# A cross-attention and mixture-of-experts kernel on one core: the order of all steps made anew, without a limit on how close GpSimd's transfers stand

## The chip, the core and the metric

The kernel runs on one core of a Trainium2 chip. Its engines run beside each other, each in the order of its own queue, and wait for one another by semaphores: TensorE (PE; its weight loads are shown as PEld), VectorE (DVE), ScalarE (ACT), GpSimd (POOL) and SyncE (SP), which here issues transfers only. GpSimd issues the indirect transfers, whose target rows are read from memory. The metric is the device time of one execution in microseconds (us), less is better. A profile is one more execution, recorded instruction by instruction.

## What is computed

A layer norm, cross-attention of 2 x 1024 tokens to 2 x 154 context rows with 16 heads of 16, a residual sum, a second layer norm, and a mixture of 8 experts of which each token takes the best two. All is in 32-bit floats. The reference, cut:

```python
x = x + attention(layernorm(x), ctx, ctx, Wq, bq, Wk, bk, Wv, bv, Wo, bo)
x = x + ffn(layernorm(x), router_w, w1, w2)

def ffn(x, router_w, w1, w2):            # 2048 tokens of 256
    probs = softmax(x @ router_w.T)      # 8 experts
    vals, idx = top_k(probs, 2)
    out = zeros_like(x)
    for eid in range(8):
        w = sum(where(idx == eid, vals, 0), axis=-1)
        out = out + w[:, None] * (gelu(x @ w1[eid].T) @ w2[eid].T)   # 256 -> 1024 -> 256
    return out
```

## The kernel before

**Stages.** The 2048 tokens lie in four blocks of 512 (numbers 0 to 3). For each block there is attention: `prep_norm`, `flip_half` and `prep_q` make the queries; `maxima` (L618 on TensorE, L625 on VectorE) finds each row's largest score; `drop` sends these by SyncE through a small DRAM buffer into the queries' spare rows (L642, L645); `exps` and `last_exps` make the exponentials (scores on TensorE L657 and L674, exponentials on ScalarE L663 and L680); `values` (L695, L703), `divide`, and `project` (L735, L742) finish it, and `project` also stores the block's sum into `out`. Then the block's tokens are normed again into two buffers `xn` of half a block each (`second_norm` L767), and `logits`, `share`, `choose` and `place` find each token's two experts and its row in a table `row_d` in DRAM. `pack` (L776) puts the shares beside the rows in `xn`.

**The scatter.** `record.n.i` takes the 128 tokens i of block n: VectorE casts their two row numbers (L867), and GpSimd issues two indirect transfers that write the 128 rows of 1,088 bytes from `xn` into `row_d` (L874). So a block has four `record` steps and eight transfers. `fill` writes rows of nobody behind each expert's last row, also from GpSimd. A later fetch of rows waits for all scatters ahead of it in the program, and a later scatter for the reads of the fetches ahead of it. Rows of `xn` can't be written again until the scatters have read them.

**The experts.** The table is worked through in tiles of 128 rows, all of one expert. `plan.1` picks the first nine tiles from the counts of blocks 0 and 1, `plan.0` the others from all four; its last part also plans "quarter tiles", of four groups of 32 rows with an expert each, which take up what is left over (L913 to L945). For tile j SyncE fetches the expert's weights w1 (`fetch_weights`, L1100; for quarter tiles L1112) and the rows (`fetch_rows`, L1124; L1128 for quarters), TensorE turns the rows (`flip_rows`, L1137), VectorE copies the result to `xgT` (L1140), `expand` is the first matmul (L1181, for quarters L1195) with a GELU on ScalarE (L1186), and `contract` the second (L1247), after which VectorE weighs the result into one of three buffers `ag` (L1273) and GpSimd adds its rows into `out` by an indirect transfer (L1276). w1 has room for five tiles, rows for three, `xgT` for two. The experts' second weights w2 lie in a buffer for all eight (`load_w2`, L281); its last two places serve as scratch for the attention before they are loaded.

**The order.** The steps are generators: each `yield` ends a part. A list `ORDER` of 710 words, written out by hand or by a planner outside the file, names the step whose next part is issued next. As TensorE, VectorE, ScalarE and SyncE take their instructions in that order, the list sets each queue. GpSimd does so only up to the step `release`; after it, its own order is chosen when the kernel is built, from the same program. TensorE's results go to PSUM, with three places of one kind ("two", for `maxima` and `exps`, two places each, and `last_exps` and `expand`, one each) and two of another ("one", for most other steps). After `ORDER` a loop (`tiles`) goes on from tile 13 to the last, the same in both kernels.

The loop that issues the list:

```python
    for word in ORDER.split():
        name, *args = word.split(".")
        advance(name, *[int(a) if a.isdigit() else a for a in args])
```

Of the kernel before, what the change touches and what calls it, by code (L numbers as in the profile page):

```python
# [52 lines left out]
warm first_moments.0 first_moments.0 first_moments.0 loads.x1 biases first_moments.0  # L53
first_scale.0 biases prep_norm.0 prep_norm.0 prep_norm.0 prep_norm.0 loads.wq first_moments.1
constants flip_context.1 flip_context.0 first_moments.1 flip_context.1 flip_context.0
first_moments.1 flip_half.0.0 flip_half.0.0 flip_half.0.1 flip_half.0.1 keys.0 prep_q.0.0
first_moments.1 loads.x3 loads.bo first_scale.1 loads.wv keys.0 last_context.0 loads.wo
last_context.1 keys.0 keys.1 first_offset.1 prep_q.0.0 first_moments.3 prep_q.0.0
first_moments.3 prep_norm.1 keys.1 maxima.0.0 maxima.0.0 keys.1 first_offset.0 maxima.0.0
last_values.1 prep_norm.1 load_w2.4 last_values.1 maxima.0.1 prep_norm.1 last_values.1  # L60
maxima.0.1 loads.bias loads.rw first_moments.3 prep_q.0.1 clear_last prep_q.0.1 loads.x2
more_keys.0 maxima.0.1 maxima.0.2 maxima.0.2 prep_q.0.1 more_keys.1 maxima.0.3 load_w2.1
context_values.0 context_values.1 maxima.0.3 prep_norm.1 context_values.0 maxima.0.2 release
context_values.0 maxima.0.3 context_values.1 flip_half.1.0 drop.0.0 context_values.1
first_moments.2 maxima.0.4 flip_half.1.0 drop.0.0 flip_half.1.1 flip_half.1.1 flip_output
more_keys.0 flip_output maxima.0.4 prep_q.1.0 last_values.0 prep_q.1.0 first_moments.2
prep_q.1.0 maxima.0.4 first_moments.3 exps.0.0 exps.0.0 maxima.0.5 maxima.0.5 maxima.0.5
exps.0.0 centred_router last_values.0 maxima.0.6 maxima.0.6 last_values.0 exps.0.1 maxima.0.6
exps.0.1 centred_router maxima.0.7 maxima.0.7 values_bias values_bias maxima.0.7 exps.0.1
drop.0.1 first_moments.2 prep_q.1.1 first_scale.3 prep_q.1.1 last_exps.0.0 maxima.1.0  # L70
output_router last_exps.0.0 prep_q.1.1 maxima.1.0 more_keys.1 maxima.1.1 maxima.1.0
output_router values.0.0 first_offset.3 maxima.1.1 first_moments.2 drop.0.1 values.0.0
values.0.0 values.0.0 maxima.1.1 first_scale.2 exps.0.2 exps.0.2 first_offset.2 exps.0.2
own_logits.0 values.0.0 own_logits.0 prep_norm.3 prep_norm.3 maxima.1.2 maxima.1.2 output_bias
prep_norm.2 maxima.1.3 maxima.1.2 last_exps.0.1 maxima.1.3 maxima.1.3 prep_norm.2 exps.0.3
prep_norm.2 drop.1.0 drop.1.0 prep_norm.2 own_logits.1 last_exps.0.1 output_bias own_logits.1
flip_half.2.0 flip_half.2.0 output_bias divide.0.0 output_bias exps.0.3 exps.0.3 values.0.1
divide.0.0 values.0.1 values.0.1 values.0.1 exps.1.0 flip_half.2.1 exps.1.0 maxima.1.4
values.0.1 divide.0.1 exps.1.0 maxima.1.4 prep_norm.3 divide.0.1 maxima.1.5 maxima.1.5
project.0.1 maxima.1.4 maxima.1.6 maxima.1.5 maxima.1.6 flip_half.2.1 exps.1.1 maxima.1.6  # L80
exps.1.1 maxima.1.7 prep_q.2.0 exps.1.1 maxima.1.7 last_exps.1.0 maxima.1.7 add_bias.0 drop.1.1
drop.1.1 prep_q.2.0 last_exps.1.0 project.0.1 maxima.2.0 prep_q.2.0 project.0.0
second_moments.0.1 maxima.2.0 maxima.2.1 maxima.2.0 second_moments.0.1 project.0.0 maxima.2.1
prep_norm.3 load_w2.2 maxima.2.1 load_w2.5 values.1.0 values.1.0 second_moments.0.0 values.1.0
values.1.0 exps.1.2 exps.1.2 maxima.2.2 second_moments.0.0 logits.0 values.1.0 exps.1.2
maxima.2.2 maxima.2.3 prep_q.2.1 maxima.2.2 logits.0 last_exps.1.1 maxima.2.3 second_scale.0
prep_q.2.1 load_w2.3 clear_last prep_q.2.1 own_logits.2 maxima.2.3 second_scale.0 drop.2.0
add_bias.1 logits.0 last_exps.1.1 divide.1.0 own_logits.2 logits.0 divide.1.0 exps.1.3 share.0
values.1.1 share.0 exps.1.3 values.1.1 exps.1.3 share.0 drop.2.0 values.1.1 values.1.1 exps.2.0
second_norm.0 choose.0 last_exps.2.0 exps.2.0 exps.2.0 choose.0 place.0 maxima.2.4 values.1.1  # L90
place.0 last_exps.2.0 maxima.2.4 maxima.2.4 flip_half.3.0 flip_half.3.0 flip_half.3.1 maxima.2.5
flip_half.3.1 pack.0 prep_q.3.0 record.0.0 maxima.2.5 maxima.2.5 divide.1.1 maxima.2.6
record.0.0 maxima.2.6 exps.2.1 exps.2.1 maxima.2.6 prep_q.3.0 divide.1.1 maxima.2.7 exps.2.1
prep_q.3.0 maxima.2.7 project.1.1 maxima.2.7 maxima.3.0 drop.2.1 record.0.1 record.0.1
project.1.1 logits.1 add_bias.2 second_norm.0 project.1.0 drop.2.1 maxima.3.0 second_moments.1.1
logits.1 maxima.3.1 maxima.3.0 second_moments.1.1 project.1.0 record.0.2 second_moments.1.0
# [1409 lines left out]
```

## Time and profile before

| | us |
|---|---|
| median of 3 runs | 423.14 |
| lowest and highest run | 419.65, 423.66 |
| the profiled execution | 419.35 |
| its span, first to last instruction | 417.6 |
| its TensorE busy, VectorE busy | 396.0, 209.4 |
| granted TensorE clock | 0.995 |

The page says how long each engine was busy, cuts the span into 40 slices of some 10.4 us with a digit for the busy tenths of each, and lists groups of instructions with what ended the idle time ahead of them. A timeline has start, duration, engine, line, operation, output and inputs, how many were merged, and in brackets the idle time ahead and its releaser. A list of waits has total, number of times, and longest. The attention of the four blocks takes the span's first 150 us, the experts the rest; choosing and scattering of blocks 2 and 3 lie beside the first experts' tiles, up to 215 us.

Transfers in `row_d` issued by GpSimd (L874), in the view of that line: 32 of rows and two of filler, 957 to 1502 ns each, 962 in the middle.

### The profile page before, as it was taken

To read this page: it belongs to the slowest core of one execution; us is meant where nothing else is said; L and a number is where in the kernel's file an instruction comes from. 1 tells how busy PE (TensorE), PEld (TensorE's weight loads), DVE (VectorE), ACT (ScalarE), POOL (GpSimd) and SP (SyncE) were. 2 spreads that over 40 slices of the span, in tenths; PEclk is the share of its full clock that TensorE was granted. 3 is DMA by queue.
4 is the path that set the end of the run, shared out by engine and by line. 5 is a ranking of instruction groups with operands and counts; after the bars stand their busy time and mean duration, and the time that the engine had idled before them with its cause. 6 is when DMAs were issued, how large, how long until landed. Compare 5 with 4: busy or idle time off the path is not lost. (4 is left out here: it accounts for less than half of the span.)

```text
span 417.6 us, 8418 instructions
## 1 busy us (share of the span) xinstructions
PE 396.0 (95%) x3018; PEld 285.2 (68%) x3018; DVE 209.4 (50%) x608; ACT 125.0 (30%) x223; POOL 112.8 (27%) x146
## 2 busy tenths in 40 slices
PE   7999999999989979999989999999999999999990
PEld 6554444335324349999979999689968977896890
DVE  5765787888888785545202313532451424234300
ACT  2556654275263446431121112111111111111110
POOL 8500080203223303345541122211311222213121
PEclk9999999999999999999999999999999999999997
DMA  7700000801456369775949988798689679876211
GB/s 242 305 10 7 3 9 8 316 9 35 167 160 221 96 229 321 237 214 156 281 100 281 316 242 242 210 368 231 174 263 366 175 199 305 301 205 200 55 19 18
DMA packets 35870, 76.19 MB, mean 182 GB/s; under 512 B 6023, under 2 KB 15921, under 8 KB 34801
## 3 DMA queue, kind: packets, MB, share of 16 engines
q1 hardware_dynamic: 28960, 66.10, 48.1%
q0 software_dynamic: 6384, 8.92, 10.2%
q8 instruction: 27, 0.44, 0.4%
q10 hardware_dynamic: 481, 0.58, 0.4%
q14 instruction: 18, 0.15, 0.1%
HBM read 63.91 MB, written 11.82 MB: 181 GB/s over the span
## 5 line engine op out<-in xcount | busy, mean ns | idle before, releaser
L1181 PE MATMUL hp<-xgT,w 128*128 128x128 f32 x928 | 110.9, 276 | 0.5 <-DVE xgT L1140 0.5
L1181 PEld LDWEIGHTS hp<-xgT,w 128*128 128x128 f32 x928 | 108.4, 192 | 4.0 <-issue 1.8
L1247 PE MATMUL yp<-w_sb,hT 128*128 x464 | 105.5, 379 | 0.0
L1276 POOL DMA_INDIRECT out_dram<-ag,ents x33 | 53.2, 1611 | 161.8 <-DMA out_dram<-ag,ents 44.2
L1247 PEld LDWEIGHTS yp<-w_sb,hT 128*128 128x128 f32 x464 | 85.8, 190 | 10.4
L1186 ACT ACTIVATE hT<-hp 128x512 f32<-128x512 f32 x58 | 33.9, 597 | 173.7 <-PE hp L1181 173.7
L625 DVE TENSOR_REDUCE nmx<-mx 128x4 f32<-128x616 f32 x64 | 48.6, 793 | 16.8 <-PE mx L618 16.4
L1140 DVE COPY xgT<-xgt 128x256 f32<-128x256 f32 x33 | 14.0, 423 | 82.8 <-PE xgt L1137 82.8
L874 POOL DMA_INDIRECT row_d<-xn,rows_i x32 | 32.0, 999 | 66.7 <-ACT xn L776 16.7
L663 ACT ACTIVATE et<-st 128x1024 f32<-128x1024 f32 x32 | 31.3, 1022 | 34.4 <-PE st L657 34.2
L1273 DVE TENSOR_SCALAR ag<-yp,ents 128x256 f32<-128x256 f32 x29 | 14.0, 483 | 46.2 <-PE yp L1247 44.1
L618 PE MATMUL mx<-kmx,q 32*128 32x308 f32 x256 | 33.4, 465 | 3.9 <-ACT et L663 3.2
L618 PEld LDWEIGHTS mx<-kmx,q 32*128 32x128 f32 x256 | 14.3, 183 | 21.2 <-ACT et L663 7.8
L657 PE MATMUL st<-q,kaug 32*128 32x512 f32 x128 | 22.9, 635 | 0.3 <-ACT et L663 0.2
L601 POOL TENSOR_TENSOR x_sb<-x_sb,bo 128x1024 f32<-128x1024 f32 x4 | 9.8, 2470 | 45.4 <-DVE bo L553 33.3
L1137 PE MATMUL xgt<-ident,xg 128*128 128x128 f32 x66 | 12.9, 277 | 3.5 <-DMA xg<-row_d 3.5
L368 PE MATMUL qp<-w_sb,wq 128*128 128x512 f32 x32 | 15.9, 619 | 0.2 <-ACT w_sb L359 0.2
L703 PE MATMUL av<-et,vaug 128*32 128x512 f32 x128 | 16.0, 600 | 0.0
L735 PE MATMUL op<-wo,catT 128*128 128x256 f32 x64 | 16.0, 390 | 0.0
L1195 PE MATMUL hp<-w,xgT 128*32 128x512 f32 x128 | 15.4, 598 | 0.0
L657 PEld LDWEIGHTS st<-q,kaug 32*128 32x128 f32 x128 | 6.8, 183 | 12.4 <-issue 5.8
L1231 DVE COPY x_sb<-w_sb 128x1024 f32 x16 | 11.4, 714 | 6.9 <-issue 6.6
(224 smaller groups left out, 378.5 us busy)
## 6 DMA issues: line engine op xcount, KB each, us to landing
w<-in_w_dram SPq DMA_DIRECT2D x90, 512.0 KB
w_sb<-in_w_dram SPq DMA_DIRECT2D x8, 1024.0 KB
xg<-row_d SPq DMA_DIRECT2D x29, 136.0 KB
out_dram<-x_sb SPq DMA_DIRECT2D x8, 256.0 KB
x_sb<-in_x_dram SPq DMA_DIRECT2D x3, 512.0 KB
xg<-row_d SPq DMA_DIRECT2D x16, 34.0 KB
out_dram<-ag,ents POOLq DMA_INDIRECT x33, 6.3
x_sb<-in_x_dram SPq DMA_DIRECT2D x2, 256.0 KB
```

What stands on the lines that cost most here:

```text
L368: nc.tensor.matmul(qp, wq_sb[:, dc, c * P : (c + 1) * P], xnT[:, dc, :], start=dc == 0, stop=dc == DC - 1,)
L618: nc.tensor.matmul(sc[j // 2][:, j % 2, 0 : 2 * SC], q[r, 0, i * P : (i + 1) * P], kmx[c][r, b].rearrange("r g s -> r (g s)"), start=True, ...
L625: nc.vector.tensor_reduce(out=nmx[c][:, i, 0 : 2 * QJ].rearrange("p (g j) -> p j g", g=2)[:, pair * 2 : pair * 2 + 2, :], in_=sc[pair][:, ...
L657: nc.tensor.matmul(st[j // 2][:, j % 2, :], kaug[r, b, g, 0:SM], q[r, g % 2, :], start=True, stop=True)
L663: nc.scalar.activation(et, st[pair], AF.Exp)
L703: nc.tensor.matmul(av[gg][j * QR : (j + 1) * QR, :], vaug[:, b, g, j, :], state["et", n, g, j // 2][:, j % 2, :], start=False, stop=True,)
L735: nc.tensor.matmul(op[:, ii, :], catT[:, c, i * P : (i + 1) * P], wo_sb[:, c, :], start=c == 0, stop=c == DC - 1,)
L874: ins = nc.gpsimd.indirect_dma_start(out=row_d, out_offset=bass.IndirectOffsetOnAxis(ap=to, axis=0), in_=row, in_offset=None,)
L1181: nc.tensor.matmul(hp[:, q, :], w1t[dc][:, hc * P : (hc + 1) * P], xgT[:, dc, :], start=dc == 0, stop=dc == DC - 1,)
L1186: nc.scalar.activation(hT[:, half * (HC // 2) : (half + 1) * (HC // 2), :], hp, AF.Gelu)
L1247: nc.tensor.matmul(yp, hT[:, hc, :], w2_flat[:, bass.ds(state["e", j] * (HC * D) + hc * D, D)], start=hc == 0, stop=hc == HC - 1,)
L1276: nc.gpsimd.indirect_dma_start(out=out[0 : reach(j), :], in_=to, in_offset=None, out_offset=row_of(j), bounds_check=reach(j) - 1, oob_is_e ...
```

## The change

Only the list `ORDER` is another. It has the same 710 words, each as often as before. In the earlier list GpSimd's transfers were kept apart; the new one was made without that limit, so that the four `record` steps of a block can stand close to each other. All other steps were placed anew as well.

The diff, cut to the places of which most is said (words are in the list's order; a word stands once for each part of its step):

```diff
-maxima.3.6 record.1.1 project.0.0 exps.3.1 divide.2.1 divide.2.1 maxima.3.7 own_logits.3
-exps.3.1 maxima.3.7 project.2.1 maxima.3.7 project.0.1 logits.2 project.2.1 pack.1 drop.3.1
-record.1.1 load_w2.7 second_norm.1 last_exps.3.0 logits.2 record.1.2 plan.1 record.1.2
-last_exps.3.0 project.2.0 drop.3.1 second_moments.2.1 plan.1 project.2.0 values.3.0 values.3.0
-plan.1 record.1.3 record.1.3 second_moments.2.1 values.3.0 values.3.0 exps.3.2 fetch_weights.0
-last_exps.3.1 exps.3.2 exps.3.2 second_moments.2.0 values.3.0 second_moments.2.0 last_exps.3.1
-fetch_rows.0 second_scale.2 exps.3.3 exps.3.3 divide.3.0 values.3.1 fetch_weights.1 values.3.1
...
-contract.7.0 flip_rows.9 fetch_rows.10 contract.4.1 expand.8.0 flip_rows.9 fetch_weights.10
-fetch_weights.11 contract.7.1 contract.7.1 expand.9.0 expand.8.1 expand.9.1 flip_rows.10
...
-flip_rows.12 fetch_weights.14 expand.11.0 expand.10.1 fetch_weights.13 expand.11.1 contract.9.1
-flip_rows.13 plan.0 contract.8.1 expand.11.1 contract.10.0 contract.10.1 expand.11.0
...
+maxima.3.6 exps.3.1 pack.1 logits.2 own_logits.3 exps.3.1 exps.3.1 second_norm.1 record.1.1
+maxima.3.7 plan.1 maxima.3.7 record.1.1 project.2.0 maxima.3.7 record.1.2 drop.3.1 drop.3.1
+plan.1 record.1.2 project.2.1 project.2.0 last_exps.3.0 record.1.3 last_exps.3.0 project.2.1
+record.1.3 plan.1 second_moments.2.0 second_moments.2.1 values.3.0 add_bias.3 fetch_weights.0
+second_moments.2.0 values.3.0 last_exps.3.1 second_moments.2.1 exps.3.2 last_exps.3.1 values.3.0
+second_scale.2 fetch_rows.0 values.3.0 second_scale.2 values.3.0 divide.3.0 divide.3.0
+fetch_rows.1 exps.3.2 exps.3.3 exps.3.2 exps.3.3 project.1.0 values.3.1 logits.2 exps.3.3
...
+contract.7.1 contract.7.1 fetch_rows.9 fetch_rows.11 contract.5.1 contract.8.0 flip_rows.9
+contract.8.1 fetch_rows.10 fetch_weights.10 flip_rows.9 contract.8.1 expand.9.0 flip_rows.10
...
+fetch_rows.14 contract.10.1 expand.12.0 expand.12.1 flip_rows.13 expand.12.0 fetch_weights.13
+project.3.1 contract.10.1 contract.11.0 flip_rows.13 contract.11.1 expand.12.1 expand.13.0
+expand.13.1 contract.12.0 contract.8.1 plan.0 contract.11.1 contract.9.1 expand.13.1
```

By engine, TensorE's list differs little: most steps are moved by one to four places. In the new list `last_exps.2.1` stands before `exps.2.3`, `flip_rows.0` and `flip_rows.1` together ahead of `expand.0.0` and `project.3.0`, `place.2` after `project.3.1` (it was ahead of `expand.0.1`), `flip_rows.7` after `expand.6.0`, `flip_rows.8` after `expand.7.1`, and `flip_rows.9` between the halves of `contract.8`. On VectorE the cast of `record.1.3` stands ahead of `plan.1`'s second part, and the last part of `plan.0` behind `contract.10.1` and `flip_rows.13`. On ScalarE `pack.1`'s second part stands ahead of `exps.3.1`, and `pack.3`'s first part ahead of the GELU of `expand.3.0`. On SyncE `load_w2` steps and the stores of `project` change places with `drop`, and the store of `project.3.1` is the list's last.

## The prediction

> **What bounds the kernel now.** I read the page first (busy shares, and the 40 slices), then TensorE's waits, then the timelines of TensorE, GpSimd, SyncE and VectorE around those waits. The page's chain of waits is no help: it holds only the last GpSimd transfer.
>
> ```profile
> PE 396.0 (95%) x3018; PEld 285.2 (68%) x3018; DVE 209.4 (50%) x608; ACT 125.0 (30%) x223; POOL 112.8 (27%) x146
> PE   7999999999989979999989999999999999999990
> DVE  5765787888888785545202313532451424234300
> ```
>
> TensorE (PE) is the bound from end to end; VectorE (DVE) comes near it only in the attention half. Time can come only from TensorE's gaps. Its waits, with what released them (total, times, longest):
>
> ```profile
> PE xgt L1137 <- DMA xg<-row_d: 3.5, 2, 1.8
> PE mx L618 <- ACT et L663: 3.2, 5, 0.7
> PE hp L1181 <- DVE xgT L1140: 0.5, 1, 0.5
> ```
>
> The largest is `flip_rows` (L1137) waiting for gathered rows, twice. TensorE's timeline shows where:
>
> ```profile
> 146.95 2.14 PE L703 MATMUL av<-et,vaug 128*32 128x512 f32 x16
> 150.91 0.41 PE L1137 MATMUL xgt<-ident,xg 128*128 128x128 f32 x2 [1.83 <-DMA xg<-row_d]
> 151.16 2.17 PE L735 MATMUL op<-wo,catT 128*128 128x256 f32 x8
> 153.86 2.05 PE L1181 MATMUL hp<-xgT,w 128*128 128x128 f32 x16 [0.53 <-DVE xgT L1140]
> 219.48 0.41 PE L1137 MATMUL xgt<-ident,xg 128*128 128x128 f32 x2 [1.71 <-DMA xg<-row_d]
> ```
>
> What SyncE's queue waited for before it could fetch those rows, and GpSimd's timeline, with the last transfers of block 1 (each `record` is a pair) and four of block 3:
>
> ```profile
> SPq L1124 <- DMA row_d<-xn,rows_i: 30.6, 4, 10.0
> SPq L1124 <- DMA row_d<-nobody_u,at_i: 14.7, 1, 14.7
> SPq L1078 <- DVE qwhich_i L945: 6.1, 1, 6.1
> ```
>
> ```profile
> 136.25 0.99 POOL L874 DMA_INDIRECT row_d<-xn,rows_i  x1 [3.35 <-issue]
> ...
> 142.16 0.96 POOL L874 DMA_INDIRECT row_d<-xn,rows_i  x1 [3.67 <-issue]
> 143.43 0.96 POOL L874 DMA_INDIRECT row_d<-xn,rows_i  x1 [0.30 <-issue]
> ...
> 203.05 1.00 POOL L874 DMA_INDIRECT row_d<-xn,rows_i  x1 [0.30 <-ACT hT L1186]
> 204.35 0.98 POOL L874 DMA_INDIRECT row_d<-xn,rows_i  x1 [0.30 <-issue]
> ...
> 206.90 0.96 POOL L874 DMA_INDIRECT row_d<-xn,rows_i  x1 [0.30 <-issue]
> ```
>
> Pairs of block 1 start at 124.84, 130.38, 136.25 and 142.16, five to six us apart; four transfers in a row at 203 keep a step of 1.29 us. So the spacing is the order's, not the engine's. A second kind of loss isn't listed as a wait: between starts on TensorE's timeline a `maxima` right behind an `exps` takes 2.0 to 2.3 us instead of 0.73. Taking each kind's usual start-to-start time as its price, the attention half (to 149) loses about 25 us so.
>
> **The change part by part.** It is a permutation: the same 710 words, so no instruction is added or removed. I sorted both lists by engine.
>
> *TensorE* keeps nearly its old order; every landmark has the same work before it, to within a step or two. The differences before 149, priced from before's own adjacent pairs: `last_exps.2.1` moves from behind `exps.2.3` to before it (it cost 1.25 extra; I put 0.2). `values.2.0`'s last part no longer stands between `maxima.3.2` and `maxima.3.3` (0.5 lost). From `place.1` (122.20) to the end of `values.3.1` before loses 6.1 us; the new adjacencies come to 1.5 (`exps.3.0`/`maxima.3.4`) + 0.4 + 0.8 (`maxima.3.6`/`exps.3.1`) + 0.6 + 1.2 (`values.3.0` right behind `last_exps.3.0`) + 0.7 = 5.2. Gain 1.05 - 0.5 + 0.9, rounded down to 1.0; bounds 1 lost to 2 gained, as each pair is uncertain by some tenths.
>
> *GpSimd's scatters, block 1.* In VectorE's list the cast of `record.1.3` stood behind `plan.1`'s second part (DVE 138.66 to 141.33); now it stands before that part and before one projection, and `plan.1`'s matmul comes about 3 us earlier. With `record.1.2` freed by `second_norm.1` near 134, four transfers at 1.29 (from 203) take 134.2 to 139.3, against 144.4. A transfer lands 2.4 to 7.8 us after issue (median 3.9), so rows can be fetched by about 141 to 145 instead of 148.75, and TensorE reaches `flip_rows.0` near 148 (in before its work ahead ends at 147.83 + 0.97 = 148.8, less the attention's gain). The 1.83 wait goes. What is late next is VectorE: `flip_rows.0` and `.1` and `expand.0.0` now follow each other, so `expand.0.0` waits for the copy of `xgT` (about 0.85), and `project.3.0` behind it for `divide.3.1` (three operations, 1.75 us: 0.5). Before loses 2.9 here (2.11 + 0.80 over the usual pitch), after 1.35: gain 1.6, bounds 0 and 2.4.
>
> A rule speaks against runs of scatters. Row first: 32 record transfers took 0.96 us in the middle, 1.50 at most, beside a VectorE that is 80% busy. The Trainium skill, "SBUF — State Buffer", section "SBUF: two separate sides", says that GpSimd can't write its descriptors while VectorE runs a two-port operation, fp32 copies between SBUF tiles above all, and is blocked to that operation's end. By the rule four transfers would each lose up to one VectorE operation (0.7, the row of L709): 2.8 us, more with more held operations, rows at 148, half the entry's gain gone, sum 2.3 instead of 3.1. By the row it costs nothing. I take the row, since these very transfers ran beside the same VectorE work.
>
> *Fill, and `flip_rows.9`.* The filler rows leave at 212.84 and 214.12 and SyncE fetches at 216.77. `fill` keeps its place (behind `contract.5.1` on VectorE), but `flip_rows.9` moves from inside `contract.7` to inside `contract.8`: 3.46 us of matmuls later (two halves of 1.73). The 1.71 wait is covered even if the fill comes 1.7 us late; gain 1.8, bounds 0 and 1.9. `fetch_weights.10` follows those rows on SyncE: I expect it issued near 216.5, landing near 222.5, wanted at 224.9. `flip_rows.7` and `.8` move back by 5 to 7 us too, so their fetches have more slack.
>
> *`plan.0`'s last part* moves back on VectorE, behind `contract.10.1` and `flip_rows.13`. It took 2.4 us and ended at 239.79; now it starts with `flip_rows.13`, near 244, and ends near 246.5. SyncE's list behind it in before, and TensorE's first matmul of the quarter tile:
>
> ```profile
> 240.30 4.41 SPq L1112 DMA_DIRECT2D w<-in_w_dram  x4
> 245.72 3.02 SPq L1128 DMA_DIRECT2D xg<-row_d  x4
> 249.64 1.68 SPq L1112 DMA_DIRECT2D w<-in_w_dram  x2
> 254.19 1.71 SPq L1112 DMA_DIRECT2D w<-in_w_dram  x2
> ```
>
> ```profile
> 265.02 1.92 PE L1195 MATMUL hp<-w,xgT 128*32 128x512 f32 x16
> ```
>
> Started at 247.0 with the same steps, the quarter rows leave at 252.4 to 255.4 behind 2 MB of weights (6 to 7 us at the 300 GB/s of these slices) and land near 258; TensorE, 4 us early, wants them near 257.2. The last weights leave at 260 to 261.6, land near 264.4, wanted at 263.2 (267.29 less 4.1). I put 1.3 us lost, bounds 0 and 4 (all that was gained).
>
> *Other moves on SyncE*: `load_w2` and the `project` stores change places with `drop`'s small transfers; each load goes out when its target is free, several us from the next `drop`, hidden by TensorE's queue: zero, 1 us if a `drop` falls behind 1 MB. `project.3.1`'s store, now last, holds the scatter of `contract.9`; three `ag` buffers and 7.2 us a tile cover it. After tile 14 both kernels run the same code, TensorE full.
>
> **Sum**: 1.0 + 1.6 + 1.8 - 1.3 = 3.1 us. The profiled execution took 419.35 (span 417.6, 1.75 around it), so it would take 416.25; the median of the runs is 3.79 above it, and I apply the same difference there: 423.14 - 3.1 = 420.0.
>
> **Rivals.** *More gain*: the quarter tile hides its late plan (1.3 back), the entry gains 2.4 and attention 2: 6.1 to 6.6, about 416.8. For it: the attention half has 25 us of loss to take from. Against it: TensorE's pairs hardly change. *Nothing*: the cover is eaten, fill late by 2 to 3 us and `fetch_weights.10` behind it (1.2 + 1.1), attention 1 worse: about 423. For it: the landings reach 7.8 us when weights are in flight (DMA 0.99 busy at 200 to 210). *Slower*: ScalarE is held by the row buffers. There are two `xn` halves; `pack.1`'s second copy now stands ahead of `exps.3.1` on ScalarE, and `pack.3`'s first ahead of the GELU of `expand.3.0`; both wait until a run of scatters has read its half. With landings of 2.4 both have some 3.3 us of slack. If a run of eight lands in 10.4 (the 7.8 and half of four more steps of 1.29), each loses 10.4 - 2.4 - 3.3 = 4.7: 9.4 lost, 3.1 gained, about 429. It decides from landings of 9.4 on. Against it: 7.8 is the most seen, and the pairs of block 0 mostly land alone. That the change does nothing to the spacing is partly so: block 3's pairs still wait for ScalarE and for `contract.5.1`.
>
> **How the numbers follow.** About 1% (4.2 us) is what a measurement of this kernel can tell from no change. Main case 0.45 (0.10 of it faster by over 1%); more gain 0.25 (0.23 faster); nothing 0.15 (0.04 slower, the rest same); ScalarE held 0.15 (0.13 slower). That makes 0.33 faster, 0.50 same, 0.17 slower. The main case alone spans 418 to 422; 414.5 to 427 leaves out some 0.08 below and 0.11 above.
>
> **What would show it.** Right: `record.1.3` ends before 140.5, SyncE fetches first rows before 146, TensorE lists no wait over 1 us at `flip_rows.0` and `.9`, and 0.5 to 2 us appear at the quarter tile's L1137 or L1195. Wrong: scatters over 1.5 us each, ScalarE's `xn` copies waiting for `row_d`, or TensorE's loss before 149 changed by over 3 us.

## The result, and the profile after

The changed kernel took 434.0 us in the median of four runs (431.53 to 436.93), the kernel before, beside it, 423.4: a ratio of 1.029 with a 95% interval of 1.020 to 1.037. It is slower, where I forecast a gain of 0.7%. On two more chips the ratio came out as 1.027 [1.019, 1.034] and 1.021 [1.010, 1.032], on a third as 1.016 [1.012, 1.021]; the difference between the chips is part of what follows. Medians here are of all runs, ratios are of the runs in the faster of two states that executions fall into. The profiled execution took 431.53 us, its span is 429.8.

From the page of the changed kernel, the busy shares and the slices that the prediction showed of the kernel before, and one row more, the granted clock of TensorE in tenths:

```profile
PE 401.9 (94%) x3018; PEld 285.0 (66%) x3018; DVE 212.5 (49%) x608; ACT 123.3 (29%) x221; POOL 110.0 (26%) x146
PE   8999899999989599999998999899999999999990
DVE  5785896897968576546212133332252244133300
PEclk9999989999988699999999999999999999999996
```

and that last row on the page of the kernel before:

```profile
PEclk9999999999999999999999999999999999999997
```

TensorE is busy 5.9 us longer with the same 3018 matmuls, and the clock row has an 8 in slice 6 (54 to 64 us) and 8, 8 and 6 in slices 12 to 14 (118 to 150 us), the last of which also has TensorE idle for half its time. The work is the same, so both are losses. TensorE's waits in the changed kernel (total, times, longest):

```profile
PE av L695 <- ACT er L680: 4.9, 1, 4.9
PE xgt L1137 <- DMA xg<-row_d: 2.9, 2, 1.8
PE pp L853 <- DVE took L835: 1.4, 1, 1.4
PE mx L618 <- ACT et L663: 1.3, 2, 0.7
```

The first was 1.2 us in the kernel before, and the third is not in its list:

```profile
PE av L695 <- ACT er L680: 1.2, 1, 1.2
```

TensorE's timeline at the three places the prediction named, and at the first tile whose weights come in quarters:

```profile
157.59 0.44 PE L1137 MATMUL xgt<-ident,xg 128*128 128x128 f32 x2
158.76 2.05 PE L1181 MATMUL hp<-xgT,w 128*128 128x128 f32 x16
160.65 1.89 PE L735 MATMUL op<-wo,catT 128*128 128x256 f32 x8
...
229.69 0.41 PE L1137 MATMUL xgt<-ident,xg 128*128 128x128 f32 x2 [1.84 <-DMA xg<-row_d]
...
270.41 0.41 PE L1137 MATMUL xgt<-ident,xg 128*128 128x128 f32 x2 [1.05 <-DMA xg<-row_d]
271.07 3.69 PE L1247 MATMUL yp<-w_sb,hT 128*128 x16 [0.25 <-PE xgt L1137]
274.69 1.92 PE L1195 MATMUL hp<-w,xgT 128*32 128x512 f32 x16
279.20 1.90 PE L1195 MATMUL hp<-w,xgT 128*32 128x512 f32 x10 [0.25 <-DMA w<-in_w_dram]
```

At the entry (157.59) the wait for rows is gone. At `flip_rows.9` (229.69) it is as long as before. At the quarter tiles TensorE waits, and loses more than the listed waits: from the start of `contract.12.0` to the end of the span the old trace takes 163.4 us, this one 169.0. (The new order has `flip_rows.14` behind `contract.12.0`, so 0.2 us of the 5.6 is work that only changed sides.)

To see where the rest lies I walked TensorE's steps in both traces and took from each its kind's usual start-to-start time, as the prediction did for the attention half. The sums by stretch, in us of loss (the last column is a duration), with traces of later runs beside them:

```
                          start to  flip_half.1.0  place.1 to   last_exps.3.0  flip_rows.0  expand.7.0      contract.12.0
                          flip_     to place.1     last_        to flip_       to expand.   to contract.    to the end
                          half.1.0                 exps.3.0     rows.0         1.0          12.0
before                      4.2       13.3           4.2          4.2            1.0          2.2             163.4
after                       1.5       17.9           5.7          7.4            0.9          2.1             169.0
after, on chip D (e15)      2.9       18.4           4.1          1.9            0.9          1.4             168.0
old order (e11)             2.4       13.3           4.2          2.3            2.9          2.5             163.7
new order mended (e13)      4.2       15.3           4.1          2.9            0.9          4.2             163.4
```

So the end of the loss is at the quarter tiles (5.6 us), and the rest in the attention half: from `flip_half.1.0` to `last_exps.3.0` (6.1) and from there to the first gathered rows (3.2). The experiments take these apart.

### The profile page after: what moved, and what is told of

Read it like the earlier page. It is cut to its first block, busy times and chain, and to the rows that moved or that the text cites. A ratio compares the mean times of both kernels' runs of the same rounds, so it can differ in the third digit from the quotient of the medians.

```text
span 429.8 us, 8421 instructions
## 1 busy us (share of the span) xinstructions
PE 401.9 (94%) x3018; PEld 285.0 (66%) x3018; DVE 212.5 (49%) x608; ACT 123.3 (29%) x221; POOL 110.0 (26%) x146
## 3 DMA queue, kind: packets, MB, share of 16 engines
q0 software_dynamic: 6384, 8.92, 10.8%
## 5 line engine op out<-in xcount | busy, mean ns | idle before, releaser
L1276 POOL DMA_INDIRECT out_dram<-ag,ents x33 | 51.8, 1571 | 174.6 <-DVE ag L1273 72.4
L1140 DVE COPY xgT<-xgt 128x256 f32<-128x256 f32 x33 | 13.9, 421 | 71.8 <-PE xgt L1137 66.6
L874 POOL DMA_INDIRECT row_d<-xn,rows_i x32 | 31.2, 974 | 49.2 <-issue 12.2
L657 PE MATMUL st<-q,kaug 32*128 32x512 f32 x128 | 24.4, 659 | 0.2
L703 PE MATMUL av<-et,vaug 128*32 128x512 f32 x128 | 18.7, 678 | 0.0
L1195 PE MATMUL hp<-w,xgT 128*32 128x512 f32 x128 | 17.4, 599 | 0.2 <-DMA w<-in_w_dram 0.2
L709 DVE STREAM_TRANSPOSE u<-av 128x512 f32<-128x512 f32 x16 | 11.2, 705 | 9.6 <-PE av L703 9.4
L695 PE MATMUL av<-er,vrem 32*32 32x512 f32 x128 | 11.0, 665 | 5.0 <-ACT er L680 4.9
```

The costliest lines, as they stand in the source:

```text
L657: nc.tensor.matmul(st[j // 2][:, j % 2, :], kaug[r, b, g, 0:SM], q[r, g % 2, :], start=True, stop=True)
L703: nc.tensor.matmul(av[gg][j * QR : (j + 1) * QR, :], vaug[:, b, g, j, :], state["et", n, g, j // 2][:, j % 2, :], start=False, stop=True,)
L874: ins = nc.gpsimd.indirect_dma_start(out=row_d, out_offset=bass.IndirectOffsetOnAxis(ap=to, axis=0), in_=row, in_offset=None,)
L1195: nc.tensor.matmul(hp[r, :], xgT[:, dc, r], w1t[half * Q4 + i][:, dc, :], start=dc == 0, stop=dc == DC - 1,)
L1276: nc.gpsimd.indirect_dma_start(out=out[0 : reach(j), :], in_=to, in_offset=None, out_offset=row_of(j), bounds_check=reach(j) - 1, oob_is_e ...
```

## The experiments

Eighteen runs were made in five groups, each group on one chip with the kernel before beside it; six of them repeat a kernel. I call the chips A to E: A for e1 to e4 (the kernel before took 419.5 us there), B for e5 to e8 (423.5), C for e9 to e12 (419.4), D for e13 to e15 (419.4), E for e16 to e18 (424.6). Every edit but e4's moves words of the list only; `word(2)` stands for the second part of a step.

### Which half of the order, and the plan: e1 to e4 (chip A)

```diff
 e1: old list up to flip_rows.0, then what is left of the new list, in its order
 e2: new list up to flip_rows.0, then what is left of the old list
 e3: new list, one word moved
-contract.12.0 contract.8.1 plan.0(4) contract.11.1
+flip_rows.12(2) plan.0(4) fetch_rows.14 contract.10.1
 e4: new list; matmuls of constants whose result is overwritten:
+4 of 128x128 in flip_half.2.0, 12 of 128x32 in place.1, 12 of 128x128 in values.3.0
```

> The new order with everything up to the first flip of gathered rows (flip_rows.0) put back into the old order; from there on the new order stands. The two traces differ by 6.7 us at that place and by 12 us at the end. Theory A (TensorE's lulls in the attention part of the new order, and the granted clock that falls to half after them, make most of the loss): the front gives back 6 to 7 us, so 427 us (425 to 429) and a granted clock of 1.0 from 14 us to the last tile. Rival B (the loss is made behind the entry, by late rows and the late plan): 433 us, since the front gives back under 2 us.

> The reverse: the new order up to flip_rows.0, the old order behind it. Theory A: 430 us (428 to 432), with windows of half clock between 50 and 150 us. Rival B: 424 us.

> The new order with one word moved: the last part of plan.0 stands right behind the copy of flip_rows.12, ahead of contract.10.1, in place of behind contract.8.1. If the late plan costs what the windows from 260 to 280 us show (2.5 us of TensorE's time): 431.5 us, and no wait of over 0.5 us at the quarter tiles. If the quarter tiles' waits are made good later by a TensorE that is ahead: 434 us. The front is that of the new order, so this run also shows whether the 4.9 us wait of values.3.0 for the softmax of last_exps.3.0 comes again: theory A says that it does, at 140 to 147 us.

> The new order, with matmuls on constants that nobody reads added where TensorE stands still in the trace: 4 of 128x128 ahead of flip_half.2.0, 12 of 128x32 ahead of place.1, 12 of 128x128 ahead of values.3.0 (about 1.0, 1.0 and 3.2 us of work in lulls of 1.2, 2.4 and 4.9 us). If the half clock follows from the lulls and costs time by itself: no window of half clock before the last tile, and 429 us (427 to 431). If the clock follows something else or its loss lies in waits anyway: 434 to 437 us, with the same windows of half clock.

Measured, beside 419.5: e1 428.39 (ratio 1.022 [1.016, 1.028]), e2 425.44 (1.011 [1.006, 1.016]), e3 421.74 (1.002 [0.998, 1.006]), e4 432.07 (1.027 [1.021, 1.033]).

e3 is the find: one word of 710 brings the new order to within 2.2 us of the kernel before. (e15 puts the changed kernel itself at 5.5 us over it on such a chip, so the word is worth some 3 by the medians, and some 6 by the ratios, 1.002 and 1.016.) So much of the loss is behind the entry, against my theory A. e1, which has the old front, says the same with its tail, but not with its time: in its trace 6.4 us more than before are lost between `flip_rows.0` and `expand.1.0`, at the joint of the two lists, where neither list loses them. The tail from `contract.12.0` took 169.0 us in e1, 168.4 in e4, 164.0 in e2 and 165.2 in e3. e2 does not fit so well: with the old tail it still took 1.1% more than the kernel before. Three of its ten runs lie at 419.4 to 420.0 us with a mean granted clock of 0.983 to 0.990, the other seven at 423.8 to 426.5 with 0.973 to 0.981. The trace is of a run of the first kind, so where the others lost their time is open. The chain behind the word, in the changed kernel's timeline (VectorE's last steps of `flip_rows.13`, the first and last operation of the plan, and the transfer that needs its result):

```profile
253.94 0.42 DVE L1140 COPY xgT<-xgt 128x256 f32<-128x256 f32 x1 [3.30 <-PE xgt L1137]
254.61 0.14 DVE L1033 SCALAR_TENSOR_TENSOR filled<-qend,end 1x1 int32<-1x1 f32 x1
...
257.15 0.17 DVE L945 CAST qwhich_i<-qwhich 128x12 int32<-128x12 f32 x1
257.88 0.66 SPq L1112 DMA_DIRECT2D w<-in_w_dram  x1
```

The last operation of `plan.0` ended at 239.79 before and ends at 257.32 here. It waits on VectorE behind the copy of `flip_rows.13`, and that copy waits 3.30 us for TensorE's `flip_rows.13`, which the new list puts behind the whole of `expand.12`. The first quarter weights leave at 257.88 in place of 240.30: 2.9 us ahead of the start of `contract.12.0` (260.77) in place of 13.9 (254.22).

e3 also refutes half of its own expectation: the 4.9 us wait of `values.3.0` did not come again. The stretch from `last_exps.3.0` to `values.3.0` took 2.27 us, with the same list up to there. e4's expectation fell whole: the time was 432.07 us, and half clock came at 34.7 to 41.5 and 130.3 to 140.5 us.

### The late plan in the old order, and GpSimd's runs: e5 to e8 (chip B)

```diff
 e5: the changed kernel as it is
 e6: old list
-flip_rows.13 plan.0(4) contract.8.1
+contract.12.0 plan.0(4) contract.12.1
 e7: e3, and
-expand.13.1(1) ... flip_rows.14(1) ... expand.13.0(2) flip_rows.14(2)
+expand.13.0(1) flip_rows.14(1) flip_rows.14(2) expand.13.1(1)
 e8: old list
-record.1.1(2) ... record.1.2(2) ... record.1.3(1) record.1.3(2)
+record.1.1(2) record.1.2(2) record.1.3(1) record.1.3(2)
-record.2.0(2) ... record.2.1(2) ... record.2.2(2)
+record.2.0(2) record.2.1(2) record.2.2(2)
```

> The changed kernel as it is, on the chip of the other runs, for a figure of its own beside them. In the runs so far the span times the granted clock (the time less what the half clock took) is 412 to 413 us for the kernel before and for the new order with the early plan, and 418 to 419 us wherever the plan stands late. Theory A (the late plan costs about 6 us, the half clock the rest of the 11 to 12): 428 to 433 us, and 417 to 419 us of span times clock in every run. Theory C (the 12 us are the clock alone, drawn by chance, and the late plan costs the 2.5 us that show as waits): 424 us in the median here, and runs of 420 among them.

> The old order with one word moved the other way: the last part of plan.0 from ahead of contract.8.1's scatter to behind contract.12.0, where the new order has it. Theory A: 5 to 6 us over the kernel before (ratio 1.012 to 1.015), and the first matmul of the quarter tiles' weights waits for its weights. Theory C: 2.5 us (ratio 1.006).

> The new order with the last part of plan.0 early, as before, and both parts of flip_rows.14 put ahead of expand.13.1, where the old order has them: the 0.91 us wait of expand.14 for its rows goes, and the quarter tiles take the 163.4 us from contract.12.0 to the end that they take in the old order, in place of 165.2. 1.5 us under the run with the early plan alone: 420 us, span times clock 410.5. If it shows no gain over the kernel before, the front's gain of 4 us is eaten by the half clock; then span times clock is at least 1.5 us below that of the kernel before.

> The old order with nothing changed but GpSimd's transfers: record.1.1, 1.2 and 1.3 stand as six transfers in one run, and record.2.0, 2.1 and 2.2 as another, each at the place of its last but one in the old order. If a run costs nothing by itself (each transfer holds GpSimd 0.96 us in a run as out of one): within 1 us of the kernel before. If a run slows what shares the queues with it (the small stores and loads of the maxima, the first rows): 2 to 4 us slower, with a longer wait of last_exps.3.0 or flip_rows.1.

Measured, beside 423.5: e5 435.58 (1.027 [1.019, 1.034]), e6 432.36 (1.017 [1.009, 1.025]), e7 429.17 (1.014 [1.010, 1.017]), e8 424.02 (0.999 [0.995, 1.003]).

e6 settles that the plan's place costs time: in the old order, too, one word costs 1.7%, some 7 us. It doesn't settle the price in the new order, since the plan is later here: it ends 1.9 us behind the start of `contract.12.0`, in the changed kernel 3.5 us ahead of it. e6's tail took 173.5 us, 10 more than the old one's; 6.83 us of it ran at half clock, behind a window in which TensorE had no matmul at all, so at most 3.4 of the 10 are the clock. Over the other traces the tail is 167.4 to 169.4 us with the plan late (after, e1, e4, e5, e9, e15, e16, e17), and 163.4 to 164.1 with plan and `flip_rows.14` as the old list has them (before, e2, e7, e8, e10, e11, e13, e14, e18). e3 and e12, with only the plan early, have 165.2 and 165.1: of about 5 us, 3.3 are the plan's and 1.5 are `flip_rows.14`'s, whose copy stands late on VectorE (0.2 of it are its own matmuls, which stand behind `contract.12.0` now).

e7 mended the tail (164.1 us) and still lost, so theory A is incomplete. e8 shows what the change's few words amount to: nothing within 0.4% either way. The edit did less than its expectation says: GpSimd's own order is the same in e8 as in the kernel before, so moving its words changes nothing, and only the one word of VectorE, the cast of `record.1.3`, made four transfers out of two and two.

e5 and e7 brought the wait of `values.3.0` back: 5.47 and 5.85 us from `last_exps.3.0` to `values.3.0`. The changed kernel's timeline shows what is odd in it (GpSimd, TensorE and ScalarE around the place; "remote" is a release that the profile can't assign to an instruction):

```profile
139.08 0.96 POOL L874 DMA_INDIRECT row_d<-xn,rows_i  x1 [0.30 <-DVE til L990]
140.17 1.09 PE L674 MATMUL sr<-q,kaug 32*32 32x512 f32 x16
140.35 0.96 POOL L874 DMA_INDIRECT row_d<-xn,rows_i  x1 [0.30 <-issue]
...
142.87 0.96 POOL L874 DMA_INDIRECT row_d<-xn,rows_i  x1 [0.30 <-issue]
145.09 1.02 ACT L680 ACTIVATE er<-sr 128x1024 f32<-128x1024 f32 x1 [7.41 <-remote]
146.17 1.11 PE L695 MATMUL av<-er,vrem 32*32 32x512 f32 x8 [4.91 <-ACT er L680]
```

The matmuls of `last_exps.3.0` end at 141.26. ScalarE's exponential, which waits for nothing else, starts at 145.09, and TensorE's release is on record at 145.07, 3.8 us late and 1.2 us after GpSimd had written the last of six transfers. In e3 the same six transfers lie over the same step, and ScalarE starts at once:

```profile
141.00 0.96 POOL L871 DMA_INDIRECT row_d<-xn,rows_i  x1 [0.30 <-issue]
141.28 1.09 PE L671 MATMUL sr<-q,kaug 32*32 32x512 f32 x16
142.26 0.96 POOL L871 DMA_INDIRECT row_d<-xn,rows_i  x1 [0.30 <-issue]
142.48 1.02 ACT L677 ACTIVATE er<-sr 128x1024 f32<-128x1024 f32 x1 [3.95 <-PE sr L671]
143.53 0.96 POOL L871 DMA_INDIRECT row_d<-xn,rows_i  x1 [0.30 <-issue]
```

So the list alone doesn't bring the late release; the chip has a part in it. A second mark goes with it: in the traces of chips B and E and of the changed kernel's first run, many of VectorE's releases are missing from the record (22 to 53 of some 500; 43 of 501 in the changed kernel's first run), most of them in stretches in which GpSimd writes transfers. TensorE's own are among those that are missing (352 records for 366 releases in the changed kernel's first run). On A, C and D at most two of VectorE's are missing, and in the first trace of the kernel before none. The two traces that I compared first may thus be from chips of two kinds.

### Splitting the run, and making one in the old order: e9 to e12 (chip C), e16 to e18 (chip E)

```diff
 e9, e16: new list
-record.1.3(1) last_exps.3.0(2) project.2.1(2) record.1.3(2) plan.1(3)
+last_exps.3.0(2) project.2.1(2) plan.1(3) record.1.3(1) record.1.3(2)
 e10: the same in e7
 e11, e18: old list
-record.1.2(1) record.1.2(2) ... record.1.3(1) record.1.3(2)
+record.1.1(1) record.1.2(1) record.1.3(1) ... record.1.2(2) ... record.1.3(2)
 e12: e3 a second time; e17: the changed kernel as it is
```

> The new order with both words of record.1.3 (VectorE's cast of its rows and GpSimd's transfers) moved from around last_exps.3.0 to behind the last part of plan.1: the run of six transfers at the softmax of the remainder becomes four, a pause, two. In three traces (the changed kernel, its second run, the new order with plan and flip_rows.14 early) TensorE's release of last_exps.3.0 came 3.3 to 3.8 us after its last matmul, 1.2 to 1.6 us after the last transfer of the run had been written; in two others of another chip it came at once under the same run. Theory M (a release waits there for the end of GpSimd's run): on a chip that shows it, the release comes within 1.6 us of the fourth transfer, values.3.0 starts 2.3 to 3.6 us behind last_exps.3.0 in place of 5.5 to 6.0, and the time falls by 2 to 3 us against the changed kernel, to 431 to 433 us. Rival D (the wait belongs to the small loads of drop.3.1, which are under way in the same microseconds): 5.5 to 6.0 us again and 434 to 436 us.

> The same move in the new order with plan.0 and flip_rows.14 early. It ran at 429.2 us where the kernel before ran at 423.5. Theory M: 426 us on such a chip; on one that does not show the late release, no change from the run with the early plan, 420 to 421 us beside 419.5 of the kernel before.

> The mirror in the old order: VectorE's casts of record.1.2 and record.1.3 stand right behind that of record.1.1, so that GpSimd writes the six transfers from about 130.5 to 138.5 us without a pause, across the end of last_exps.3.0 (135.9 us). Theory M: on a chip that shows the late release, values.3.0 starts 2 to 3 us later than in the old order and the time grows by 2 to 3 us. Rival D, or a chip without it: within 1 us of the kernel before.

> The new order with the early plan alone, a second time, beside the others on their chip. On a chip without the late release it ran at 421.7 us against 419.5. Theory M: on a chip with it, 3 to 4 us more than the kernel before's own difference between the chips, 429 us; the trace then shows 5.5 to 6.0 us from last_exps.3.0 to values.3.0 in place of 2.3.

On chip C, beside 419.4: e9 428.72 (1.021 [1.014, 1.029]), e10 422.57 (1.008 [1.004, 1.011]), e11 420.22 (1.002 [0.998, 1.006]), e12 422.33 (1.005 [1.001, 1.009]). This chip does not show the late release: 2.27, 2.27, 3.17 and 2.49 us at the place. So e9 and e11 told nothing of theory M there, e12 repeated e3, and e9 against e12 is 6.4 us, not all of it the late plan: of 5.7 us between the two traces 2.3 lie in the tail and 1.8 ahead of `flip_half.1.0`. They ran again on chip E:

> The new order with record.1.3 behind plan.1, a second time. Theory M (the release waits for the end of the run): on a chip where the changed kernel beside it shows 5.5 to 6.0 us from last_exps.3.0 to values.3.0, 2.3 to 3.6 us here. Rival D (the small loads of drop.3.1): 5.5 to 6.0 us. On a chip that shows 2.3 us in both, nothing is told.

> The changed kernel as it is, to tell which kind of chip this is: 6.0 us from last_exps.3.0 to values.3.0 and 434 to 436 us, or 2.3 us and 424 to 426 us.

> The old order with the casts of record.1.2 and 1.3 early, a second time. Theory M, on a chip with the late release: values.3.0 starts 2 to 3 us later behind last_exps.3.0 than the 3.2 us of the kernel before. Rival D: 3.2 us.

Measured, beside 424.6: e16 429.54 (1.012 [1.000, 1.023]), e17 433.04 (1.021 [1.010, 1.032], two runs), e18 424.09 (1.001 [0.996, 1.006]). Chip E is of the late kind. The mirror is the clearest: in e18 the old order has a run over `last_exps.3.0`, and ScalarE is held. From its timeline, 135.85 being the end of the matmuls:

```profile
134.56 0.96 POOL L871 DMA_INDIRECT row_d<-xn,rows_i  x1 [0.30 <-issue]
134.76 1.09 PE L671 MATMUL sr<-q,kaug 32*32 32x512 f32 x16
135.82 0.96 POOL L871 DMA_INDIRECT row_d<-xn,rows_i  x1 [0.30 <-issue]
137.09 0.96 POOL L871 DMA_INDIRECT row_d<-xn,rows_i  x1 [0.30 <-issue]
138.26 1.16 SPq L642 DMA_DIRECT2D q<-nm_d  x2
139.01 1.02 ACT L677 ACTIVATE er<-sr 128x1024 f32<-128x1024 f32 x1 [5.53 <-PE op L732]
```

It starts 3.2 us after the matmuls and 1.0 after the run; in the old order without that run, on chip B (e6, e8), the stretch took 3.16 us, here 5.33, as theory M has it. All six traces with the run on a chip of the late kind, from the release to the two things it could wait for:

```
                                   after    e5      e7      e16     e17     e18
release                            145.07  148.15  146.90  145.54  146.61  138.99
behind the end of GpSimd's run       1.2     1.2     1.6     1.2     0.5     0.9
behind the start of q's loads        3.3     2.5     5.2     2.4     5.1     0.7
```

The release keeps close to the end of the run, and not to the loads of `drop.3.1`: rival D falls. In e18 a second release of TensorE was held over the same run: matmuls that ended at 136.16 let VectorE's copy (L960) start at 139.05. What is not shown: whether the recording, which loses releases in the same stretches, has a part in it; why only some chips do it, and why other releases inside the same run come in time (VectorE's addition at 140.28 follows its matmuls by 0.04 us in the changed kernel). Nor does the price follow simply. e16 is 3.5 us under e17, as forecast, but 3.0 against 3.3 us at the place is not where that came from, since e17's run had itself broken up; and e18 loses 2.2 us at the place and ends level with the kernel before.

### The half clock: e13 to e15 (chip D)

The granted clock by windows, the changed kernel first (stretch; length and TensorE's busy time, with its matmuls; granted clock; share and GB/s of the DMA engines):

```profile
51.10:54.50 3.40, 2.32 (x28) 1.00 0.40 46
54.50:58.00 3.50, 3.50 (x28) 0.51 0.74 302
122.80:126.20 3.40, 1.54 (x24) 1.00 0.84 347
126.20:133.10 6.90, 6.75 (x44) 0.51 0.56 192
139.90:143.30 3.40, 1.36 (x18) 1.00 0.31 110
143.30:150.10 6.80, 3.93 (x32) 0.50 0.66 205
```

The trace of the kernel before has 1.00 in all of these. The steps of the clock lie on a grid of 3.41 us with another phase in each execution. 17.07 us at half clock between the start and the last tile can cost up to 8.5 us of TensorE's work, and less where it waits anyway. TensorE's busy share before each drop is 0.68, 0.46 and 0.40, but idle time isn't the measure. In 20 traces I counted, for each window of the grid at full clock from 13 to 400 us, the columns that the matmuls starting in it streamed, each weighted by the share of the array (rows times columns) that it used:

```
columns in the window     windows    followed by half clock
under 1000                   12          12
1000 to 1500                 29          14
1500 to 2000                123           2
over 2000                  2057           0
```

TensorE's busy share parts the same windows less well: half clock came behind 12 of 13 that were busy for under half of the time, 5 of 53 from 0.5 to 0.7, and 10 of 135 from 0.7 to 0.85. One window with TensorE busy throughout was followed by half clock: e4's at 126.9, which my own fillers of 32 columns had filled, 960 weighted columns in all. This is one reason why e4 failed; its other half clock, at 34.7 us, is in a place that I had not filled. The Trainium skill, "TensorE: Matmul & The Clock Gate", section "Part 1: The HAM clock gate (the "warmup" mystery)", describes such a free-running window of about 3.4 us and puts the half rate behind an idle one. The grid and the half rate are as it says; here an idle window was not needed, and the count above decides.

By that count a stretch without an idle window is at risk: from 30 to 37 us, where the `maxima` use 32 of 128 rows. In 11 of the 12 traces with the new front there is a window of half clock between 33 and 58 us, in none of the 6 with the old front. It is a risk and no more: windows of 1468 columns in that stretch or just ahead of it were followed by half clock in e9, e12, e15 and e16, and not in the kernel before, e8 and the changed kernel's first run. What decides between 1000 and 1500 is open. e13 puts a large step there.

```diff
 e13: e10, and e14: the old list; one word moved in both
-last_values.0(1) behind maxima.0.7(1) (new list), behind prep_q.1.0(1) (old list)
+exps.0.0(2) last_values.0(1) maxima.0.5(1)
 e15: the changed kernel as it is
```

> The new order with plan.0 and flip_rows.14 early and record.1.3 late, and one more word moved: the matmuls of last_values.0 (four of 128x256 columns, 0.96 us) from behind maxima.0.7 to ahead of maxima.0.5, into the stretch from 30 to 37 us that holds nothing but small steps, and where TensorE waits 1.28 us for ScalarE. If little streamed work in a window is what halves the clock (theory A): no half clock between 30 and 42 us, 3.5 to 4.5 us less of loss there, and 417.5 to 419 us where the same order without the move ran at 422.6 beside 419.4. If the half clock comes by chance: again 422 us, less at most 1 us for the wait that is filled.

> The old order with the same word moved to the same place, ahead of maxima.0.5. The old order has no half clock there, so only the 1.28 us wait can be filled: 0.5 to 1 us under the kernel before if nothing later takes it back, 0 if the wait of exps.0.1 for ScalarE grows by as much.

> The changed kernel as it is, a third time. On a chip without the late release of last_exps.3.0: that stretch takes 2.3 us in place of 6.0, and by the runs with the plan late (6.4 us over the early plan) 428 to 430 us beside 419.5; on a chip with it 434 to 436 us beside 423.5.

Measured, beside 419.4: e13 420.23 (1.003 [1.000, 1.005]), e14 421.60 (1.002 [0.999, 1.006]), e15 424.89 (1.016 [1.012, 1.021]). The windows around the stretch, in e15:

```profile
29.70:33.10 3.40, 2.79 (x24) 1.00 1.01 424
33.10:40.00 6.90, 6.90 (x28) 0.51 0.13 53
```

and in e13, where TensorE is busy for as long:

```profile
30.50:33.90 3.40, 2.79 (x24) 1.00 1.00 414
33.90:40.80 6.90, 6.78 (x51) 1.00 0.24 94
```

28 matmuls in one and 51 in the other in the same 6.9 us; the window ahead holds 1468 weighted columns in e15 and 1672 in e13. In this trace the drop is gone, and the stretch from `flip_half.1.0` to `place.1` loses 15.3 us in place of 18.4. The time fell by 2.3 us against e10, from another chip but beside the same 419.4 of the kernel before; I had expected 3.5 to 4.5 for the place. Two windows at half clock cost about 3 us there, not more. Nor is the drop gone from every run: the granted clock is 0.986 in the median of e13's runs and 0.9825 in that of e10's, which is some 3 us less of half clock in a run, not 6.8. e14 missed: no gain, and in its trace 10.24 us at half clock from 125.6 on, behind a window of 1386 columns. With both of the new order's late words put right, the run split and this word moved, the new order is level with the old one. No run beat the kernel before.

## Why the prediction was wrong

Two terms of the sum failed: attention, put at 1.0 gained, and the late plan, put at 1.3 lost. On chip D, where no release comes late, the forecast was 3.1 us gained and 5.5 were lost, 8.6 off. Of these, attention is 6.0 and the tail behind the plan 3.2 (4.5 in place of 1.3); what is left nearly cancels.

**Attention** was put at 1.0 gained (bounds 1 lost to 2 gained). From `flip_half.1.0` to `last_exps.3.0` the new order lost 5.0 us more than the old one in e15, of which e13's trace gives back 3.1, where the half clock is gone; about 2 are left, which I did not trace further. The step that failed is the price: I took the pairs of steps at the cost that they had in the old trace, all of it at full clock. "TensorE's loss before 149 changed by over 3 us" was on my list of signs that would show me wrong, and it came.

**The clock** was no term of my sum at all, and so a part of those prices without my seeing it. The old trace shows 9 in all its slices but the last, and I took that as given. In these traces it held behind all 2057 windows with over 2000 weighted columns. In the attention half the new order lets single windows fall under that, and each drop costs up to half of the 3.4 or 6.8 us that follow.

**`plan.0`'s last part** did what the prediction said, and cost more. "Near 246.5" was 10.8 us too early in the trace's time (257.32), but TensorE was as late: the forecast had it 4.1 us early, with `contract.12.0` at 250.1, and it came at 260.77. So the plan ended 3.5 us ahead of `contract.12.0`, where the forecast has 3.6. The start of that step before and after, and SyncE's list behind the plan, after:

```profile
254.22 3.62 PE L1247 MATMUL yp<-w_sb,hT 128*128 x16
```

```profile
260.77 1.89 PE L1247 MATMUL yp<-w_sb,hT 128*128 x8
257.88 4.47 SPq L1112 DMA_DIRECT2D w<-in_w_dram  x4
263.39 3.34 SPq L1128 DMA_DIRECT2D xg<-row_d  x4
267.50 1.68 SPq L1112 DMA_DIRECT2D w<-in_w_dram  x2
270.90 2.10 SPq L1112 DMA_DIRECT2D w<-in_w_dram  x2
```

The last two weights have left 12.2 us behind the start of `contract.12.0`, where the forecast has 11.5. What was sized too small is the time from there to TensorE's use of them: I had 2.8 us (261.6 to 264.4), and TensorE could go on at 279.20, 6.2 us later (5.1 in e15). The rate that I had put on these slices, 300 GB/s, was too high as well: the old trace moves 245 and 248 GB/s from 240 to 260 us. Counted from the start of `contract.12.0` to the first matmul of L1210, behind the first quarter tile's `expand`, the changed kernel loses 5.3 us against the old one: 1.7 by the quarter rows, 2.2 by the last weights (0.8 and 2.0 in e15), and 1.4 by `flip_rows.14`, which I had not looked at and which e3 shows alone. Forecast for the plan 1.3 with bounds of 0 and 4, measured 3.9 in the first trace, 2.9 in e15, and 3.3 as the mean of the tails. Why the last weights took so long is not shown; the eight loads of the next experts' weights left from 274.95 on, while they were on their way.

**The entry** was right in sign and near in size where nothing else disturbs it: from `last_exps.3.0` to `expand.1.0` the old order loses 5.2 us (before and e11), the new one 2.8 (e15), a gain of 2.4 where I had 1.6 (bounds 0 and 2.4). So was the mechanism. `record.1.3` was written at 143.83 and not by 139.3, but TensorE was late by then: behind the start of `last_exps.3.0` it was written 3.7 us (3.2 in e15), against 9.6 before, and the first rows were fetched 5.9 us behind it (146.03), against 14.0 (148.75). One thing I had not seen: GpSimd's addition of a bias (L605) held the transfers back to 136.53, so that six went out in a row and not four. On the first chip the late release ate the gain: 7.4 + 0.9 of loss there against 5.2.

**`flip_rows.9`** was put at 1.8 gained. In the changed kernel the wait is 1.84 us and nothing was gained; in e15 a wait of 0.99 is left, and the stretch from `expand.7.0` on gained 0.9. I had the fill come 1.7 us late at most. `record.3.3` went out at 219.88 and the filler rows behind it at 222.43 and 223.70, 9.6 us later than before, of which 6.7 are the delay of the whole trace at `flip_rows.0`. The other 2.9 took most of the cover of 3.46 us.

**The scatters** themselves did as the prediction's row said: 0.96 us each in runs of six, so the rule of the Trainium skill that I weighed against it ("SBUF — State Buffer", "SBUF: two separate sides") cost nothing that shows. A cost of runs exists all the same, in another place: the release of a matmul that comes late on some chips.

**The rivals.** The slower one (ScalarE held by its row buffers until scatters have read them) is not what happened: no `xn` copy waits for `row_d` in ScalarE's list. The slower cases that came were SyncE's queue behind the plan, which I had priced too low, and a granted clock that does not hold, which I had in none of them.

On chip D the terms add up. e15 against the mean of the old traces (before and e11): -0.4 at the start, +5.0 in the attention half, -2.4 at the entry, about -0.6 from `expand.1.0` to `expand.7.0` (not in the table), -0.9 at `flip_rows.9`, +4.5 in the tail, together +5.2; the spans differ by 5.3, the medians by 5.5. The first trace of the changed kernel lies 7.5 us of span above e15's: 5.5 between `last_exps.3.0` and `flip_rows.0` (late release and the half clock behind it), 1.6 ahead of that from `place.1` on, 1.0 in the tail, 1.4 less at the start, and the rest in tenths.

## What to carry to other kernels

Date a step that is moved back by its distance from the step that needs its result, and not by its time in the old trace: everything between may be late together. Then price the whole way to that need, the landing of the last transfer included; here that was the part that was too short. One late word that feeds a queue of loads can cost more than all the waits that the move set out to save. When a new order makes stretches of small matmuls or short waits on TensorE, look at the granted clock by windows as well as at the busy share, and compare traces only after seeing that they show the same kind of chip.

## What the runs showed of the hardware that I had not expected

- Half clock came after all 12 windows of 3.41 us with under 1000 streamed and array-weighted columns, after 14 of 29 with 1000 to 1500, after 2 of 123 with 1500 to 2000, and after none of 2057 with more. A window that was busy throughout with narrow matmuls (960 columns, e4) was followed by it too.
- On two chips of five, and in the first run of the changed kernel, a release of TensorE to ScalarE that fell into a run of GpSimd's transfers came 0.5 to 1.6 us after the end of that run, up to 3.8 us late; on the other three the same place had it within 0.4 us.
- The kernel before took 419.4 to 419.5 us on three chips and 423.5 and 424.6 on the two with late releases: 1% between chips, more than the 0.7% that this change was expected to bring.
